# A selective scan on one NeuronCore: every fourth B product of two channel tiles moved from VectorE to ScalarE by way of a transpose, even products kept in SBUF, a third PSUM bank for the side work

## The chip, the cores and the metric

The kernel runs on one core of a Trainium2 chip. The metric is the device time of one execution in microseconds. TensorE is called PE here, VectorE DVE, ScalarE ACT, GpSimd POOL, and SyncE SP; all DMAs of the kernel are issued from SP's queue.

## The reference

The input is x, 8 images of 96 channels, 64 x 64. A vision state-space block comes first, then a small attention and a quantised feed-forward layer. What matters here is the selective scan inside the block. There are 192 inner channels (d), 16 states (n), four directions (k) over the 4,096 pixels (l), and for each of them

```python
delta = softplus(dts + dt_bias)
def step(h, inp):
    u_t, d_t, b_t, c_t = inp
    dA = exp(d_t[..., None] * A)
    h = dA * h + (d_t * u_t)[..., None] * b_t[:, :, None, :]
    y = einsum('bkdn,bkn->bkd', h, c_t)
    return h, y
```

Around the scan stand a layer norm, an input projection with a depthwise 3x3 convolution and SiLU, projections that give dts, B and C, then a norm, a gate, an output projection, two 3x3 convolutions with a channel attention, a linear attention over channels and the feed-forward layer.

## The kernel before

**The scan loop.** Images are taken in pairs (p, four of them). A pair's 2 x 192 channels are three tiles of 128 rows: T = 0 and T = 1 hold the first 128 channels of the one and of the other image, T = 2 the last 64 of both. Time runs in chunks of CH = 1,024 pixels. A *job* is one (p, direction k, chunk ci, tile T); the tiles come in the order 0, 2, 1, and there are 192 jobs. A job has four *groups* (j) of 32 channels, 768 groups in all. A group has four *units* (q = 0 to 3), and a unit is one instruction wide: its 128 partitions are 32 channels times 4 states, so that the four units hold the 16 states. Two units (q = 0, 1 or q = 2, 3) are a *pair*.

For each group PE spreads delta x (tile du, 128 channels) over channel and state: `spread` (L1299) multiplies with a 0/1 matrix into `pu`, two banks of PSUM. For each unit ACT makes da = exp(A delta) (`decay`, L1304); DVE makes the B product pb = pu x bm (L1317), where bm holds four rows of B repeated over the 32 channels; DVE scans, hc = da x h + pb (L1321); POOL copies the last column as the carry for the next chunk and multiplies hc by the C rows, cm (L1331 and the line before). `total` (L1349) adds the four states and four units on PE into `yp`; ACT copies the sum out and SP stores it, or the next direction adds to it.

`pbs` (L437) are two PSUM tiles of two banks each, pu has two, and the banks `pg` and `yp` are the two that all other work shares: eight banks. hc has eight buffers of one unit, bm four and cm five.

**The order.** Each engine's instructions are kept in the order in which the program names them (class `InOrder`; every instruction of the loop therefore has the helper's line, L266, in the profile). The loop (from L1400) goes by pairs: it runs a slot of side work, names `scan(u)`, asks for the next bm (four units ahead) and cm (two ahead), names the next pair's two `decay`, in a group's second pair also the next group's `spread` and the last group's `total`, and runs another slot. So a group has four slots and a job sixteen.

**The side work.** Everything else is written as generators, *lanes*: the projections of the next image pair, the gate, the convolutions, attention and feed-forward of the last one. `Slots` (L283) steps them once a slot. A lane takes one of the two banks with `take` (L301), which asks that a budget of PE and ACT time is positive; RATE (L291) is what each slot adds, CAP the most that is kept. `steps` (L467) prepares the next job: it loads dt rows (`st`) and du, and in slots 6 and 7 makes delta (`dls`, softplus on ACT), multiplies du by it on POOL, and stores delta.

Of the kernel before, what the change touches and what calls it, by code (L numbers as in the profile page):

```python
# [9 lines left out]
F32 = mybir.dt.float32  # L10
# [271 lines left out]

class Slots:  # L283
# [7 lines left out]
    RATE, CAP = (2.0, 1.8), (3.0, 2.4)  # L291

    def __init__(self, *banks):
        self.lanes, self.later, self.first, self.at, self.due = [], [], None, 0, {}
        self.banks, self.held, self.big = banks, set(), set()
        self.left, self.behind = [0.0, 0.0], lambda: False
# [3 lines left out]

    def take(self, pe, act, long=0):  # L301
        while True:
            i = 1 if self.at % 2 and not long else 0


            due = long and (
                self.at % 4 > (long == 2) or self.at % 16 <= 6 < self.at % 16 + long
            )
            if i not in self.held and not due and min(self.left) > (-2 if long else 0):
                self.held.add(i)  # L310
                self.pay(pe, act)
                return self.banks[i]
            yield
# [7 lines left out]
    def give(self, bank):  # L321
        i = self.banks.index(bank)
        self.after(1, lambda: self.held.remove(i))
# [4 lines left out]
    def run(self):  # L328
        self.at += 1
        self.left = [min(v + r, c) for v, r, c in zip(self.left, self.RATE, self.CAP)]  # L330
        for f in self.due.pop(self.at, ()):
            f()
        if self.first is not None and next(self.first, self) is self:
            self.first = None
        order = [self.lanes, self.later]
        for lanes in order[::-1] if self.behind() else order:
            turn = self.at % len(lanes) if lanes else 0
            for lane in lanes[turn:] + lanes[:turn]:
                if next(lane, self) is self:
                    lanes.remove(lane)  # L340

    def idle(self):
        return not (self.lanes or self.later or self.first or self.due)
# [7 lines left out]
def phase_b(  # L351
# [8 lines left out]
    with ExitStack() as ctx:  # L360
# [28 lines left out]
        gmean = cp.tile([C, C], F32, name="gmean")  # L389
        nc.vector.memset(gmean, 1.0 / (C * 128))  # L390
# [35 lines left out]
        hp = inner.enter_context(tc.tile_pool(name="b_h", bufs=8))  # L426
# [10 lines left out]
        pbs = [psc.tile([128, CH], F32, name=f"pb{i}") for i in range(2)]  # L437
# [5 lines left out]
        slots = Slots(bank0, yps)  # L443
# [6 lines left out]
        carries, bcs, dus, dls, sts, das, hcs, prevs, yet = ({} for _ in range(9))  # L450
# [11 lines left out]

        def exps():

            se.preload_act_table_set("natural_log_exp_and_others")

        def steps(job):  # L467

            p, k, ci, c, T, at = where(job)
            if T == 0:  # L470

                sts[job // 3] = gp.tile([32 + 2 * R, 512], F32, name="st")
                r0 = 64 + R * (k // 2)
                for i, hs in enumerate(halves):
                    for b in range(2):
                        nc.sync.dma_start(
                            sts[job // 3][32 * i + R * b : 32 * i + R * b + R, :],
                            xd_d[k % 2][2 * p + b][r0 : r0 + R, at][:, hs],
                        )
            dtw = gp.tile([32 + 2 * R, 128], F32, name="dtw")  # L480
            for i in range(2):
                nc.sync.dma_start(dtw[32 * i : 32 * i + 2 * R, :], a["dtw"][:, k, T, :])
            dus[job] = gp.tile([128, CH], F32, name="du", bufs=2)
            nc.sync.dma_start(dus[job], xi_d[k % 2][p][T][:, at])
            yield

            while slots.at % 16 != 6:
                yield
            dl = gp.tile([128, CH], F32, name="dls")
            for i, hs in enumerate(halves):  # L490
                bank = slots.banks[i]
                assert i not in slots.held
                slots.held.add(i)
                slots.pay(0.9, 2.5)
                rows = slice(32 * i, 32 * i + 2 * R)
                pe.matmul(bank, dtw[rows, :], sts[job // 3][rows, :], start=True, stop=True)
                se.activation(dl[:, hs], bank, AF.Softplus, bias=dtb[:, k, T : T + 1])
                slots.give(bank)
                if i:
                    exps()  # L500
                else:
                    yield
            ge.tensor_mul(dus[job], dus[job], dl)
            yield from wait(2)
            nc.sync.dma_start(dl_d[k][p][T][:, at], dl)
            yield

# [242 lines left out]
        def rest(b, s):  # L750
# [139 lines left out]
            for j in range(8):  # L890
# [17 lines left out]
                h8 = gp.tile([128, 3, 512], F8, name=f"h8{s}")  # L908
# [4 lines left out]
                for i in range(3):  # L913
                    bank = yield from slots.take(0.3, 1.3)
                    pe.matmul(bank, w1q[:, i * 128 : i * 128 + 128], x8, start=True, stop=True)
                    h16 = gp.tile([128, 512], F16, name=f"h16{s}")
# [11 lines left out]
                o16 = gp.tile([128, 512], F16, name=f"h16{s}")[0:C, :]  # L928
# [88 lines left out]
        def before_scans(p):  # L1017
# [26 lines left out]
            def norms(b):  # L1044
# [16 lines left out]
                for j in js:  # L1061
# [16 lines left out]
                    pe.matmul(bank[0:C, 0:4], gmean, cs, start=True, stop=True)  # L1078
                    se.mul(ngm, bank[0:C, 0:4], -1.0)
# [9 lines left out]
                    pe.matmul(bank[0:C, 0:4], gmean, gs, start=True, stop=True)  # L1089
                    se.activation(r, bank[0:C, 0:4], AF.Ln, bias=eps[0:C])  # L1090
# [177 lines left out]
        def weights(u, i):  # L1268
# [6 lines left out]
            if (job // 3, b, q, i) in bcs:  # L1275
                return
            t = bcp.tile([128, CH], F32, name=("bm", "cm")[i], bufs=(4, 5)[i])
            r0 = 32 * (k // 2) + 16 * i + 4 * q
            nc.sync.dma_start(
                t, xd_d[k % 2][2 * p + b][r0 : r0 + 4, at].unsqueeze(0).to_broadcast([32, 4, CH])  # L1280
# [30 lines left out]
        def scan(u):  # L1311
# [3 lines left out]
            step, last = (-1, 0) if k >= 2 else (1, CH - 1)  # L1315
            for i in range(2):
                ve.tensor_mul(pbs[i], pu, bcs[job // 3, batch(u), q + i, 0])  # L1317
            for i in range(2):
                t = hp.tile([128, CH], F32, name="hc")
                carry = carries[p, k][:, T, 4 * j + q + i : 4 * j + q + i + 1]  # L1320
                ve.tensor_tensor_scan(  # L1321
                    t[:, ::step], das.pop(u + i)[:, ::step], (pbs[i])[:, ::step],
                    0.0 if ci == 0 else carry, ALU.mult, ALU.add,
                )
                hcs[u + i] = t
            for i in range(2):
                v = u + i
                carry = carries[p, k][:, T, 4 * j + q + i : 4 * j + q + i + 1]
                if ci < NCH - 1:
                    ge.tensor_copy(carry, hcs[v][:, last : last + 1])  # L1330
                ge.tensor_mul(hcs[v], hcs[v], bcs[job // 3, batch(u), q + i, 1])  # L1331
# [17 lines left out]
        def total(g):  # L1349
# [9 lines left out]
            for n in range(4):  # L1359
                for i in range(4):  # L1360
                    pe.matmul(
                        yp[32 * i : 32 * i + 32, :], add,
                        hcs[4 * g + n][:, 256 * i : 256 * i + 256],
                        start=(n == 0 and k < 2), stop=(n == 3),
                    )
            for n in range(4):
# [33 lines left out]
        for u in range(0, n, 2):  # L1400
# [37 lines left out]
            if q == 2:  # L1438
                if g + 1 < n // 4:
                    spread(g + 1)  # L1440
                if g > 0:
                    total(g - 1)
# [504 lines left out]
```

## Time and profile before

Three runs: 11065.08, 11066.59 and 11072.03 us, median 11066.59. The profiled execution has a span of 11058.4 us from its first to its last instruction; the median is 8.2 us longer.

| engine | busy us | share of the span | instructions |
|---|---|---|---|
| PE | 7887.2 | 71% | 39468 |
| DVE | 10525.7 | 95% | 6651 |
| ACT | 6596.3 | 60% | 9175 |
| POOL | 9028.7 | 82% | 6649 |

| stretch | us | what |
|---|---|---|
| 0 to 214.6 | 214.6 | first images' norms and projections |
| 214.6 to 10724 | 10509 | scan loop |
| 10724 to 11058.4 | 334 | what is left of the last pair |

How to read it: busy is the time in which an engine had at least one instruction under way. A group's row gives the line, the engine, the operation, the tile written and those read, the shape of output and first input, the count, then the busy time, the mean ns of one instruction, and the idle time before them with what ended most of it. The mean granted clock of TensorE is 0.815 of full speed. In a timeline row come the start, the duration in us, the engine, the line, the operation and, behind x, how many instructions in a row it merges.

### The profile page before, as it was taken

To read this page: it belongs to the slowest core of one execution; us is meant where nothing else is said; L and a number is where in the kernel's file an instruction comes from. 1 tells how busy PE (TensorE), PEld (TensorE's weight loads), DVE (VectorE), ACT (ScalarE), POOL (GpSimd) and SP (SyncE) were. 2 spreads that over 40 slices of the span, in tenths; PEclk is the share of its full clock that TensorE was granted. 3 is DMA by queue.
4 is the path that set the end of the run, shared out by engine and by line. 5 is a ranking of instruction groups with operands and counts; after the bars stand their busy time and mean duration, and the time that the engine had idled before them with its cause. 6 is when DMAs were issued, how large, how long until landed. Compare 5 with 4: busy or idle time off the path is not lost.

```text
span 11058.4 us, 128094 instructions
## 1 busy us (share of the span) xinstructions
PE 7887.2 (71%) x39468; PEld 3111.6 (28%) x39468; DVE 10525.7 (95%) x6651; ACT 6596.3 (60%) x9175; POOL 9028.7 (82%) x6649
## 2 busy tenths in 40 slices
PE   7755778655568887767777787776767776665778
PEld 3322333222223332223222332223322222222223
DVE  4999999999999999999999999999999999999974
ACT  2544765544567666556776656565776656665554
POOL 2788877787898888998888887899889888988860
PEclk8877888877788888878878888887878877777889
DMA  3445554454555555666545555566544555644551
GB/s 117 151 165 180 160 156 157 141 188 156 163 185 172 171 172 157 211 214 195 158 152 160 157 178 159 177 220 209 172 157 159 160 164 179 197 157 140 173 157 37
DMA packets 900188, 1834.20 MB, mean 166 GB/s; under 512 B 247965, under 2 KB 421214, under 8 KB 892462
## 3 DMA queue, kind: packets, MB, share of 16 engines
q1 hardware_dynamic: 899502, 1826.01, 52.8%
q8 instruction: 314, 5.14, 0.2%
q14 instruction: 372, 3.05, 0.1%
HBM read 1405.13 MB, written 420.42 MB: 165 GB/s over the span
## 4 chain that ended last, share of the span: by engine, by line
PE 32%; issue 29%; DVE 17%; POOL 11%; ACT 6%; DMA 4%; SPq 0%; DVEq 0%; POOLq 0%; ACTq 0%
PE pu L266 12%; PE yp L266 11%; DVE hc L266 11%; POOL hc L266 7%; PE pg L266 6%; DVE pb L266 5%; ACT u L266 2%; ACT da L266 2%; POOL u L266 2%; PE t L266 2%; PE ps L197 1%; DMA bm<-xd 1%; POOL turn L266 1%; POOL carry L266 1%; ACT L266 1%
## 5 line engine op out<-in xcount | busy, mean ns | idle before, releaser
L266 POOL TENSOR_TENSOR hc<-hc,cm 128x1024 f32<-128x1024 f32 x3072 | 7230.0, 2359 | 591.0 <-DVE hc L266 382.6
L266 DVE TENSOR_TENSOR_SCAN hc<-da,carry,pb 128x1024 f32<-128x1024 f32 x2304 | 5276.8, 2334 | 38.1 <-ACT da L266 31.5
L266 PE MATMUL pu<-du,c_sel 128*128 128x512 f32 x3072 | 2452.5, 944 | 2244.1 <-DVE pb L266 2239.6
L266 DVE TENSOR_TENSOR pb<-pu,bm 128x1024 f32<-128x1024 f32 x3072 | 3601.6, 1220 | 133.9 <-PE pu L266 105.9
L266 ACT ACTIVATE da<-dl,c_alog 128x1024 f32<-128x1024 f32 x3072 | 3352.8, 1140 | 91.4 <-DVE hc L266 73.8
L266 PEld LDWEIGHTS pu<-du,c_sel 128*128 128x128 f32 x3072 | 790.0, 281 | 3521.1 <-DVE pb L266 2784.8
L266 DVE TENSOR_TENSOR_SCAN hc<-da,pb 128x1024 f32<-128x1024 f32 x768 | 1713.1, 2275 | 38.9 <-ACT da L266 22.8
L266 ACT COPY y<-yp 128x256 f32<-128x256 f32 x768 | 284.4, 370 | 2348.9 <-PE yp L266 2198.4
L266 PE MATMUL yp<-hc,c_add 128*32 128x256 f32 x24576 | 1660.8, 416 | 22.6 <-ACT s L266 6.6
L266 PEld LDWEIGHTS yp<-hc,c_add 128*32 128x32 f32 x24576 | 768.6, 120 | 1200.1 <-issue 628.4
L266 POOL COPY carry<-hc 128x1 f32<-128x1 f32 x2304 | 422.5, 183 | 766.1 <-DVE hc L266 744.9
L266 ACT ACT_TABLE_LOAD x566 | 726.2, 1283 | 38.2 <-DMA cb<-zs 16.9
L266 ACT COPY u<-pg 128x512 f32<-128x512 f32 (+6 forms) x397 | 218.3, 550 | 712.3 <-PE pg L266 641.2
L266 POOL TENSOR_TENSOR u<-u,u 96x512 f32<-96x512 f32 (+1 forms) x426 | 537.5, 1269 | 105.9 <-ACT u L266 101.8
L266 POOL TENSOR_TENSOR du<-du,dls 128x1024 f32<-128x1024 f32 x192 | 452.7, 2358 | 91.5 <-ACT dls L266 91.1
L266 ACT COPY u<-yp 96x512 f32<-96x512 f32 (+6 forms) x347 | 188.0, 542 | 465.5 <-PE yp L266 404.5
L266 PE MATMUL pg<-ain,wmain 96*128 96x512 f32 x792 | 354.1, 599 | 0.0
L266 PE MATMUL pg<-ain,wmix 96*128 96x512 f32 x792 | 353.0, 598 | 0.0
L266 PE MATMUL yp<-prev,ident 128*128 128x256 f32 x768 | 321.9, 512 | 39.0 <-ACT u L266 27.4
L266 PEld LDWEIGHTS yp<-prev,ident 128*128 128x128 f32 x768 | 214.5, 283 | 381.8 <-issue 264.3
L266 PE MATMUL pg<-st,dtw 12*128 12x512 f32 x384 | 218.5, 649 | 49.4 <-ACT u L266 28.8
L266 PE MATMUL yp<-st,dtw 12*128 12x512 f32 x384 | 227.9, 674 | 18.3 <-ACT u L266 10.9
(340 smaller groups left out, 7030.2 us busy)
## 6 DMA issues: line engine op xcount, KB each, us to landing
dl<-dl SPq DMA_DIRECT2D x768, 512.0 KB
bm<-xd SPq DMA_DIRECT2D x512, 512.0 KB
cm<-xd SPq DMA_DIRECT2D x512, 512.0 KB
du<-xi SPq DMA_DIRECT2D x192, 512.0 KB
dl<-dls SPq DMA_DIRECT2D x192, 512.0 KB
ya<-y SPq DMA_DIRECT2D x384, 128.0 KB
prev<-ya SPq DMA_DIRECT2D x384, 128.0 KB
xi<-u SPq DMA_DIRECT2D x152, 256.0 KB
```

What stands on the lines that cost most here:

```text
L197: nc.tensor.matmul(bank[r, :].rearrange("p (h w) -> p h w", w=W), w[:, t if len(which) > 1 or w is wmix else 0, columns], pads[b][:, 8 * j ...
L266: op(*args, **kw)
```

## The change

Tiles T = 0 and T = 1 are *woven*; T = 2 is not. In a woven group the product of the last unit (q = 3) is no longer made by DVE. B of that unit is made to be a per-partition scalar instead: `steps` loads four more rows of B for each image (`st` grows to 104 rows), and PE transposes them (into `pt`, a new bank) to `bt`, time on the partitions. Once du is there, `spin` transposes it too, 128 columns at a time, and ACT multiplies each transposed block by four columns of bt, with the four states side by side (tile `turned`, a ring of six, shared with delta). `weave` then has PE turn the part of the group back, eight transposes of 128 x 128, into the odd product's PSUM tile; it is named in a woven group's first pair, behind the next group's spread. The scan of q = 3 reads it there.

The even products' tile pb0 moves from PSUM to SBUF; pb1 stays in PSUM. That and pt leave a bank for a third lane bank, `ph`. In a woven group the third product (q = 2) is made between the first two scans, and the spread of the next group moves to the first pair. hc and cm become tiles of a pair: hc four of them (as many units as before), cm two (four units where there were five), and POOL's two products and two carry copies of a pair become one of each. Budgets rise from (2.0, 1.8) to (2.2, 2.0) a slot, and `take` picks the bank that has rested longest. The tiles h8 and h16 of the feed-forward share the buffers of others, gmean goes (its factor moves into two ACT instructions), and the program is built with dynamic_dma_scratch_size=1024.

The core of the diff:

```diff
-    RATE, CAP = (2.0, 1.8), (3.0, 2.4)
+    RATE, CAP = (2.2, 2.0), (4.0, 4.0)
...
-        hp = inner.enter_context(tc.tile_pool(name="b_h", bufs=8))
+        hp = inner.enter_context(tc.tile_pool(name="b_h", bufs=4))
...
-        pbs = [psc.tile([128, CH], F32, name=f"pb{i}") for i in range(2)]
+        bank2 = psc.tile([128, 512], F32, name="ph")
+        turning = psc.tile([128, 512], F32, name="pt")
+        pbs = [wp.tile([128, CH], F32, name="pb0", bufs=1), psc.tile([128, CH], F32, name="pb1")]
...
+        def woven(job):
+            return jobs[job][3] < 2
...
+            if T == 0:
+                bts[job // 3] = gp.tile([128, 8, 8], F32, name="bt", bufs=2)
+                yield
+                for i in range(2):
+                    r, at8 = slice(64 + 32 * i, 72 + 32 * i), 256 * i
+                    for x in range(4):
+                        pe.transpose(
+                            turning[:, at8 + 8 * x : at8 + 8 * x + 8],
+                            sts[job // 3][r, 128 * x : 128 * x + 128],
+                            ident[r, r],
+                        )
+                    se.copy(bts[job // 3][:, 4 * i : 4 * i + 4, :], turning[:, at8 : at8 + 32])
...
+        def spin(job):
+            turns[job], b = [], jobs[job][3]
+            bt, nxt = bts[job // 3], slots.at + 1
+            while len(turns[job]) < 4:
+                n, at = len(turns[job]), slots.at % 16
+                if slots.at < nxt or (job and woven(job - 1) and n >= EXTRA and 3 < at < 14):
+                    yield
+                    continue
+                nxt = slots.at + 2 - (at >= 14 or at < 3)
+                slots.pay(0.4, 2.9)
+                bank = turning[:, 256 * (n % 2) : 256 * (n % 2) + 256]
+                for i in range(2):
+                    x = 128 * (2 * n + i)
+                    pe.transpose(bank[:, 128 * i : 128 * i + 128], dus[job][:, x : x + 128], ident)
+                t = gp.tile([128, 2, 128, 4], F32, name="turned", bufs=RING)
+                for i in range(2):
+                    for m in range(4):
+                        c = 4 * b + m
+                        se.mul(
+                            t[:, i, :, m], bank[:, 128 * i : 128 * i + 128],
+                            bt[:, 2 * n + i, c : c + 1],
+                        )
+                turns[job].append(t)
+                yield
+
+        def weave(g):
+            job, j, _ = units[4 * g]
+            for x in range(8):
+                t = turns[job][x // 2][:, x % 2].rearrange("p c n -> p (c n)")
+                pe.transpose(
+                    pbs[1][:, 128 * x : 128 * x + 128], t[:, 128 * j : 128 * j + 128], ident
+                )
...
-            for i in range(2):
-                ve.tensor_mul(pbs[i], pu, bcs[job // 3, batch(u), q + i, 0])
...
+            def product(i, to):
+                ve.tensor_mul(pbs[to], pu, bcs[job // 3, batch(u), q + i, 0])
+
+            if not (woven(job) and q):
+                product(0, 0)
+                product(1, 1)
             for i in range(2):
                 ve.tensor_tensor_scan(
-                    t[:, ::step], das.pop(u + i)[:, ::step], (pbs[i])[:, ::step],
-                    0.0 if ci == 0 else carry, ALU.mult, ALU.add,
+                    t[:, i, ::step], das.pop(u + i)[:, ::step], pbs[i][:, ::step],
+                    0.0 if ci == 0 else carry[:, i : i + 1], ALU.mult, ALU.add,
                 )
...
+                if woven(job) and q == 0 and i == 0:
+                    product(2, 0)
+            if ci < NCH - 1:
+                ge.tensor_copy(carry, t[:, :, last])
+            ge.tensor_mul(t, t, bcs[job // 3, batch(u), q, 1])
...
-            if q == 2:
-                if g + 1 < n // 4:
-                    spread(g + 1)
-                if g > 0:
-                    total(g - 1)
+            if (q == 0) == woven(units[u][0]) and g + 1 < n // 4:
+                spread(g + 1)
+            if q == 0 and woven(units[u][0]):
+                assert len(turns[units[u][0]]) == 4
+                weave(g)
+            if q == 2 and g > 0:
+                total(g - 1)
```

## The prediction

> **What bounds the kernel now.** I read the page's busy times first, then the costliest groups, then the busy times of the scan loop alone (its first product starts at 214.57, its last POOL product ends near 10724), then the timeline of one stretch. From the page:
>
> ```profile
> PE 7887.2 (71%) x39468; PEld 3111.6 (28%) x39468; DVE 10525.7 (95%) x6651; ACT 6596.3 (60%) x9175; POOL 9028.7 (82%) x6649
> ...
> L266 POOL TENSOR_TENSOR hc<-hc,cm 128x1024 f32<-128x1024 f32 x3072 | 7230.0, 2359 | 591.0 <-DVE hc L266 382.6
> L266 DVE TENSOR_TENSOR_SCAN hc<-da,carry,pb 128x1024 f32<-128x1024 f32 x2304 | 5276.8, 2334 | 38.1 <-ACT da L266 31.5
> ...
> L266 DVE TENSOR_TENSOR pb<-pu,bm 128x1024 f32<-128x1024 f32 x3072 | 3601.6, 1220 | 133.9 <-PE pu L266 105.9
> ```
>
> DVE is the bound: scans and B products fill it, with little idle time before them. Busy times in the loop (columns PE, PEld, DVE, ACT, POOL, clock, DMA):
>
> ```profile
> 214.50:10724.00 10509.50, 7459.90 (x37794) 2932.34 (x37798) 10318.60 (x6150) 6404.01 (x8841) 8960.88 (x6598) 0.81 0.54 170
> ```
>
> The loop takes 10,509 us, 768 groups of four units, 13.68 us each; head and tail are the other 549. DVE's own cadence, in its timeline:
>
> ```profile
> 5003.50 4.57 DVE L266 TENSOR_TENSOR_SCAN hc<-da,carry,pb 128x1024 f32<-128x1024 f32 x2
> 5007.99 2.34 DVE L266 TENSOR_TENSOR pb<-pu,bm 128x1024 f32<-128x1024 f32 x2
> 5010.24 4.58 DVE L266 TENSOR_TENSOR_SCAN hc<-da,carry,pb 128x1024 f32<-128x1024 f32 x2
> ```
>
> Start to start, two products take 2.25 and two scans 4.49: 1.12 a product, 2.245 a scan. Scans without a carry start 2.19 apart (4.38 for two).
>
> **What decides: where the scan's inputs lie.** Today pb is in PSUM, so a scan and a product each read one tensor from SBUF, and POOL does not disturb them, though it is busy 85% of the loop: the scan with a carry has 2310/2335/2366 as its shortest, median and longest ns. The change puts the even products into SBUF; an even scan then reads two tensors there, da and pb0. The loop has no such DVE instruction, but the start of the program has. DVE's timeline, then POOL's:
>
> ```profile
> 13.56 1.47 DVE L135 TENSOR_TENSOR s<-s,tmv 128x9 f32<-128x9 f32 x1
> ...
> 15.20 1.43 DVE L128 TENSOR_TENSOR q<-q 128x9 f32<-128x9 f32 x1
> ...
> 16.83 0.10 DVE L129 TENSOR_TENSOR q<-q,tmv 128x9 f32<-128x9 f32 x1
> ```
> ```profile
> 13.38 1.63 POOL L146 TENSOR_TENSOR xt<-xt,m 128x864 f32<-128x864 f32 x1 [3.17 <-DVE m L126]
> 14.96 1.64 POOL L147 TENSOR_TENSOR xt<-xt,r 128x864 f32<-128x864 f32 x1
> ```
>
> Nine elements from two SBUF tensors take 0.10 us alone and 1.4 beside POOL, and end at 15.03 and 16.63: 0.02 and 0.03 after POOL's instructions (15.01, 16.60). A large one is put off as well: xn<-xt,tmv 128x768 takes 0.94 alone and 1.73 when it starts inside a POOL instruction, ending 0.81 after it. So such an instruction waits until the running POOL instruction is through. That DVE's turn also keeps POOL out, and that a scan behaves like a plain product, no row shows.
>
> The Trainium skill, "SBUF — State Buffer", section "Who interferes with whom", speaks against this change: any DVE instruction with two SBUF inputs and a POOL instruction that reads SBUF exclude each other for a whole instruction. By it the turns below add up; by the rows' narrower reading only plain products wait, and rival 2 holds.
>
> **The change, part by part.**
>
> *DVE's products.* Two thirds of the groups (512) lose one product: 512 x 1.12 = 575 us saved on the path as it is now. An even product written to SBUF I leave at 1.12 (the 128x768 products SBUF to SBUF run at 0.94/768 = 1.22 ns an element, the present ones at 1.19: within 0.03 either way, 0.03 x 1,024 ns = 30 ns). The scan runs at 2.2 ns an element whatever feeds it: no change of its own rate.
>
> *POOL.* A product of 512 elements takes 1.27 and one of 1,024 2.36, so 1.09 per 512 and 0.18 fixed; a pair is 0.18 + 4 x 1.09 = 4.54. 1,536 pairs = 6,973 against 7,230; carry copies halve from 2,304 to 1,152 of 0.183, saving 211. POOL in the loop: 8,961 - 257 - 211 = 8,493.
>
> *Turns.* 1,536 even scans, three quarters of 2.245 and a quarter of 2.19, are 3,427 us in which POOL may not read. If the two take turns all the time, the loop lasts 8,493 + 3,427 = 11,920 instead of 10,509. Do they? In a pair with a carry POOL holds 0.27 (carry copy, start to start) + 4.54 = 4.8; after its even scan DVE needs an odd scan and two products, 2.245 + 2.25 = 4.5, or 3.4 in the middle of a woven group. So DVE asks 0.3 to 1.4 us before POOL is done and the next pair's product lies ready behind: no time is free. Small terms: a restart of POOL after each even scan, valued at 0.1 (its gap between copy and product is 0.27 - 0.18 = 0.09; ends 0 and 0.2): 154; the gap itself, 1,152 x 0.08: 92. Turns lost to a late DVE (rival 1) in one pair of twenty: 77 x (9.3 - 7.05) = 173. Loop: 11,920 + 154 + 92 + 173 = 12,339.
>
> The low end: POOL seems to claim its turn a little after its recorded start (s<-s,tmv at 27.59 takes 0.13, although a POOL product is recorded from 27.57). With 0.1 us free in each of 1,152 + 1,536 + 1,222 = 3,910 instructions the sum falls by 391, to 11,529.
>
> *ScalarE.* 128 woven jobs x 32 = 4,096 products of 128x128 from PSUM. Rows: u<-yp 96x128 268 ns, starting 0.255 apart; u<-u,small 96x128, with a pointer operand, 0.39 apart. I take 0.36 (a pointer operand costs 0.09: turn<-turn,dsum 128x512 takes 718 ns, u<-u 96x512 without one 630), 1,475 us, between 1,044 and 1,600. ACT rises from 6,404 to 7,900 in the loop, off the path. The three products that follow one another before T = 0 stand ahead of the next da; 8.7 us of them delay a da by about 1 us, 64 times: covered by the turns, 64 us if that cover is gone.
>
> *PE.* 4,096 + 1,024 transposes; the nearest rows, four transposes of 128x96 in 0.60 or one each 0.11 us, give 0.15 each, 770 us in all, twice that at the low clock. PE rises from 7,460 to 8,230 to 9,000 of 12,339: off the path on average. The wait it adds: the last scan of a woven group waits for eight transposes (0.27 + 7 x 0.11 = 1.0, up to 2), which wait behind the spread of the next group. That one takes 1.96 at the high clock and 3.78 after a pause (the median pu matmul, 1061 ns against 590 at best, says mostly 3.78). DVE's scan before it, 2.245 plus its wait for POOL, covers this; uncovered it costs about 1 us x 512.
> The Trainium skill, "TensorE: Matmul & The Clock Gate", Part 4, says that transposes do not lift the clock and take about 275 ns each in a kernel; by that eight are 2.2 us in a row, by the rows 1.0. Neither changes the sum while POOL sets it.
>
> *Queues.* 256 more small loads of st rows, 0.32 to 0.5 us each on SP, about 100 us beside a queue that waits. cm has four buffers for five, so the first C rows of a new batch wait for POOL's last use, and later issues queue behind; 128 times between 0 and the longest such wait of now, 2.9 us (371 in all); I take 0, since POOL is one pair late anyway. Third bank, larger budgets, reused u tiles, scales moved into operands: they move lane work, which has more time per slot than before; 0, up to the 106 us that DVE waits for pu now.
>
> **Sum.** 549 + 12,339 = 12,888 of span, against 11,058; the median of the runs is 8 us above the span. Forecast 12,900.
>
> **Rivals.**
> 1. *DVE misses its turn.* When a transpose, da or spread makes DVE more than 0.3 us late, POOL starts the next pair first. Then a pair is 4.8 + 2.245 + 2.245 = 9.3 in T = 2 groups (18.6 a group); a woven group is one missed turn, 17.4 (scan, POOL's 4.8 twice, scan, product and scan: 2.25 + 9.6 + 2.25 + 1.12 + 2.25). In every group: 512 x 17.4 + 256 x 18.6 = 13,670, + 557 = 14,230; in half of them about 13,550. For: the 0.3. Against: POOL's lane work (1,222 instructions) makes POOL later, and the scan after the odd one in a woven group needs no product, so DVE is first there.
> 2. *A scan takes no turn* (faster). Place: DVE's second input; decides at all 1,536 even scans. Loop 10,509 - 575 = 9,934, + 549 + 8 = 10,490; if the cold spread delays each woven group by 1 us, 11,000. Value 10,700. For: no scan with two SBUF inputs is in the trace. Against: the rows above.
> 3. *No turns, but PE late*: the same with weave and lanes over 1.12 us a group: 11,070 to 11,400.
>
> **Chances.** Forecast 0.55, rival 1 0.26, rival 2 0.16, rival 3 0.03. The range takes in the forecast's low end (11,529 + 557 = 12,086) and rival 1 in nearly all groups: 12,050 to 14,100. Faster by over 0.2% 0.16, within 0.2% (all that a measurement here can tell from no change) 0.01, slower 0.83.
>
> **What would show it.** Right: even scans with recorded times spread from 2.3 to 7 us, odd ones constant; POOL products of 4.5 to 7; POOL plus even scans near the loop's length; ACT and PE below 75%. Wrong: even scans at 2.3 throughout. Rival 1: POOL idle for 2 us or more after most pairs.

## The result, and the profile after

The changed kernel takes 13,779.01 us (median of four runs, 13,753.90 to 13,791.22) against 11,066.63: the ratio is 1.2449, 95% interval 1.2431 to 1.2466. The profiled execution took 13,777.25 us and has a span of 13,775.5. The forecast was 12,900; the result lies 879 above it and 451 below rival 1 in every group (14,230), so nearer to the rival.

First the page of the changed kernel: the busy times, then the groups that answer to those shown of before.

```profile
PE 8978.3 (65%) x45100; PEld 3964.6 (29%) x45100; DVE 12350.5 (90%) x6138; ACT 7766.6 (56%) x13451; POOL 10863.7 (79%) x3961
...
L266 POOL TENSOR_TENSOR hc<-hc,cm 128x2048 f32<-128x2048 f32 x1536 | 7301.5, 4755 | 957.9 <-DVE hc L266 710.6
L266 DVE TENSOR_TENSOR_SCAN hc<-da,carry,pb 128x1024 f32<-128x1024 f32 x2304 | 7085.3, 3105 | 722.3 <-ACT da L266 427.5
...
L266 DVE TENSOR_TENSOR pb<-pu,bm 128x1024 f32<-128x1024 f32 x2560 | 3017.2, 1210 | 132.0 <-PE pu L266 85.6
L266 DVE TENSOR_TENSOR_SCAN hc<-da,pb 128x1024 f32<-128x1024 f32 x768 | 2223.3, 2926 | 238.2 <-ACT da L266 141.6
...
L266 POOL COPY carry<-hc 128x2 f32<-128x2 f32 x1152 | 1208.9, 1049 | 1348.1 <-DVE hc L266 1255.2
```

DVE makes 512 products fewer and is busy 1,825 us longer. The products fell by 584; the scans rose by 2,319 (a scan with a carry from 2,334 to 3,105 ns at the mean), the rest by 90. DVE's idle time, span less busy, rose from 533 to 1,425. 1,825 and 892 are the 2,717 us between the spans. A carry copy on POOL takes 1,049 ns where it took 183, for two columns.

The busy times of the scan loop (PE, PEld, DVE, ACT, POOL, clock, DMA):

```profile
226.00:13440.00 13214.00, 8546.11 (x43404) 3781.45 (x43405) 12142.44 (x5637) 7562.69 (x13083) 10797.23 (x3910) 0.78 0.44 136
```

The loop has grown by 2,705, head and tail hardly. The prediction's 8,493 us of work on POOL are recorded as 10,797: waits for a turn are recorded inside the instruction.

A stretch of T = 2, DVE's timeline and then POOL's:

```profile
5004.54 2.33 DVE L266 TENSOR_TENSOR pb<-pu,bm 128x1024 f32<-128x1024 f32 x2
5006.78 6.89 DVE L266 TENSOR_TENSOR_SCAN hc<-da,carry,pb 128x1024 f32<-128x1024 f32 x2
5013.59 2.33 DVE L266 TENSOR_TENSOR pb<-pu,bm 128x1024 f32<-128x1024 f32 x2
5015.84 6.88 DVE L266 TENSOR_TENSOR_SCAN hc<-da,carry,pb 128x1024 f32<-128x1024 f32 x2
```
```profile
5004.76 4.53 POOL L266 TENSOR_TENSOR hc<-hc,cm 128x2048 f32<-128x2048 f32 x1 [1.32 <-DVE hc L266]
5009.23 2.19 POOL L266 TENSOR_TENSOR small<-small 96x4 f32<-96x4 f32 x1
5011.38 2.36 POOL L266 TENSOR_TENSOR du<-du,turned 128x1024 f32<-128x1024 f32 x1
5013.81 4.52 POOL L266 TENSOR_TENSOR hc<-hc,cm 128x2048 f32<-128x2048 f32 x1
5022.94 4.52 POOL L266 TENSOR_TENSOR hc<-hc,cm 128x2048 f32<-128x2048 f32 x1 [4.61 <-DVE hc L266]
```

A pair lasts 9.05 us, not 6.74 as before and not 7.05 as forecast. POOL starts a pair's product as soon as the odd scan is through (5004.76). DVE's two products are done 2.25 later, and the even scan, asked for at 5006.78, stands until POOL's product ends at 5009.29. While that scan runs, four columns of 96 rows keep POOL 2.19 us: the scan shuts POOL out as well. After the odd scan it is POOL's turn again. The forecast had POOL's product run beside the odd scan and the next two products; here it runs beside the two products alone, and the even scan waits for the rest of it.

Over the whole trace the even scans are recorded at 2.26 to 12.02 us (mean 3,809 ns) and the odd ones at 2.25 to 2.35 (mean 2,313).

### The profile page after: what moved, and what is told of

It reads as the page before. It is cut to its first block, busy times and chain, and to the rows that moved or that the text cites. A ratio compares the mean times of both kernels' runs of the same rounds, so it can differ in the third digit from the quotient of the medians.

```text
span 13775.5 us, 137230 instructions
## 1 busy us (share of the span) xinstructions
PE 8978.3 (65%) x45100; PEld 3964.6 (29%) x45100; DVE 12350.5 (90%) x6138; ACT 7766.6 (56%) x13451; POOL 10863.7 (79%) x3961
## 3 DMA queue, kind: packets, MB, share of 16 engines
q8 instruction: 356, 5.83, 0.2%
## 4 chain that ended last, share of the span: by engine, by line
issue 26%; POOL 25%; PE 20%; DVE 17%; ACT 9%; DMA 3%; SPq 0%; POOLq 0%; DVEq 0%; ACTq 0%
DVE hc L266 14%; POOL hc L266 14%; PE pu L266 7%; PE yp L266 4%; POOL carry L266 4%; POOL u L266 3%; DVE pb L266 3%; PE ph L266 2%; ACT u L266 2%; ACT turned L266 2%; ACT da L266 2%; PE pb L266 2%; PE pg L266 2%; POOL du L266 2%; POOL turn L266 2%
## 5 line engine op out<-in xcount | busy, mean ns | idle before, releaser
L266 POOL TENSOR_TENSOR hc<-hc,cm 128x2048 f32<-128x2048 f32 x1536 | 7301.5, 4755 | 957.9 <-DVE hc L266 710.6
L266 DVE TENSOR_TENSOR_SCAN hc<-da,carry,pb 128x1024 f32<-128x1024 f32 x2304 | 7085.3, 3105 | 722.3 <-ACT da L266 427.5
L266 DVE TENSOR_TENSOR pb<-pu,bm 128x1024 f32<-128x1024 f32 x2560 | 3017.2, 1210 | 132.0 <-PE pu L266 85.6
L266 DVE TENSOR_TENSOR_SCAN hc<-da,pb 128x1024 f32<-128x1024 f32 x768 | 2223.3, 2926 | 238.2 <-ACT da L266 141.6
L266 POOL COPY carry<-hc 128x2 f32<-128x2 f32 x1152 | 1208.9, 1049 | 1348.1 <-DVE hc L266 1255.2
L266 ACT ACTIVATE turned<-pt,bt 128x128 f32<-128x128 f32 x4096 | 1177.7, 502 | 690.9 <-PE pt L266 336.8
L266 POOL TENSOR_TENSOR u<-u,u 96x512 f32<-96x512 f32 (+1 forms) x474 | 1009.9, 2137 | 28.2 <-ACT u L266 24.4
L266 PEld LDWEIGHTS pb<-ident,turned 128*128 128x128 f32 x4096 | 661.2, 182 | 540.3 <-DVE hc L266 296.8
L266 PE MATMUL pb<-ident,turned 128*128 128x128 f32 x4096 | 715.0, 333 | 32.7 <-DVE hc L266 32.3
L266 POOL TENSOR_TENSOR du<-du,turned 128x1024 f32<-128x1024 f32 x192 | 553.0, 2880 | 107.7 <-ACT turned L266 83.3
```

Of the source, the lines that this page charges most:

```text
L266: op(*args, **kw)
```

## The experiments

Theory T: from the even products' place in SBUF on, even scans and POOL's instructions take turns, and turns missed by DVE make the rest. Rivals are told with each run. "Busy" and "idle" are DVE's, in the profiled execution (idle is span less busy):

| kernel | us | ratio, 95% interval | busy | idle |
|---|---|---|---|---|
| before (as predicted from) | 11,067 | | 10,526 | 533 |
| after | 13,779 | 1.2449 (1.2431 to 1.2466) | 12,351 | 1,425 |
| 1 place alone | 12,795 | 1.1561 (1.1527 to 1.1594) | 11,743 | 1,049 |
| 2 no C product | 11,716 | 1.0586 (1.0555 to 1.0617) | 10,163 | 1,548 |
| 3 C product by unit | 12,899 | 1.1655 (1.1621 to 1.1689) | 11,252 | 1,647 |
| 4 scan after scan | 13,841 | 1.2505 (1.2456 to 1.2554) | 12,144 | 1,716 |
| 5 place in PSUM | 11,875 | 1.0725 (1.0707 to 1.0743) | 10,089 | 1,792 |
| 6 one woven tile | 11,432 | 1.0325 (1.0310 to 1.0340) | 10,313 | 1,122 |
| 7 no ACT products | 11,534 | 1.0420 (1.0405 to 1.0436) | 10,162 | 1,364 |
| 8 no weave | 11,454 | 1.0346 (1.0331 to 1.0362) | 10,132 | 1,333 |
| 9 decays ahead | 11,743 | 1.0607 (1.0591 to 1.0623) | 10,206 | 1,536 |
| 10 budgets alone | 11,094 | 1.0022 (1.0012 to 1.0032) | 10,527 | 561 |
| 11 one tile, decays ahead | 11,553 | 1.0436 (1.0421 to 1.0452) | 10,315 | 1,247 |
| 12 lanes before spread | 11,386 | 1.0286 (1.0269 to 1.0303) | 10,135 | 1,248 |

**1. The place alone.** The kernel before with one line of the change (and its smaller scratch for DMAs):

```diff
-pbs = [psc.tile([128, CH], F32, name=f"pb{i}") for i in range(2)]
+pbs = [wp.tile([128, CH], F32, name="pb0", bufs=1), psc.tile([128, CH], F32, name="pb1")]
```

> The kernel before with one thing changed: the even products' tile pb0 lies in SBUF instead of PSUM (and dynamic_dma_scratch_size=1024). Theory T (turns: a scan with two SBUF inputs and a POOL instruction that reads SBUF exclude each other): POOL's 8,961 us in the loop and 3,427 us of even scans add up to 12,388; with the 557 outside, 12,950 to 13,400. Rival S (the place of pb0 costs nothing; the new chains of the change, da behind the turned products and the last scan behind the transposes, make DVE late): no change, 11,030 to 11,110.

12,795 us, 155 under T's range and far from the rival: the line costs 1,727. (The smaller scratch was not run by itself, but 5 has it too, without long scans.) The busy times of its page, then a stretch of POOL's timeline:

```profile
PE 8232.4 (64%) x39468; PEld 3175.6 (25%) x39468; DVE 11743.3 (92%) x6651; ACT 6613.3 (52%) x9175; POOL 11652.5 (91%) x6649
```
```profile
5000.34 0.18 POOL L266 COPY carry<-hc 128x1 f32<-128x1 f32 x1
5000.60 2.34 POOL L266 TENSOR_TENSOR hc<-hc,cm 128x1024 f32<-128x1024 f32 x1
5002.90 2.18 POOL L266 COPY carry<-hc 128x1 f32<-128x1 f32 x1
```

One carry copy takes 0.18, the next 2.18: an even scan runs in it. POOL goes from 9,029 to 11,652 busy with the same instructions. Here the turns are used well: the median pair of T = 2 takes 7.14 us from odd scan to odd scan. The span, 12,792, is 145 below the sum of POOL's work, the even scans and the rest (8,961 + 3,427 + 549 = 12,937), 0.09 for each of the 1,536 even scans. The trace has it too: the even scans that waited (1,177 recorded above 2.6 us) end 2.15 us after the end of POOL's instruction, where two scans in a row with a carry start 2.245 apart. The prediction's low end had such an overlap.

**2. No C product.** The changed kernel without POOL's product with C.

```diff
-            ge.tensor_mul(t, t, bcs[job // 3, batch(u), q, 1])
```

> The changed kernel without POOL's product with C (hc goes to the sums unmultiplied; the carry copies, and POOL's other work stay). Theory T: POOL has some 1,500 us left in the loop, even scans fall back to a median and mean near 2.3, and the time is DVE's own sum and some waits for da and transposes: 10,500 to 11,000. Rival S: POOL is not in DVE's chain, DVE stays late: 13,200 to 13,780.

11,716: 2,063 go with the product, but 649 more than before stay, against both expectations. Against before, the products fell by 579, the scans rose by 123, the rest by 93, and the idle time by 1,015. The even products still lie in SBUF here, and the median even scan takes 2,340 ns as before: two inputs from SBUF alone do not make a scan longer. DVE's waits in this kernel (in all, times, longest; before had 54.3 for da):

```profile
DVE hc L266 <- ACT da L266: 621.9, 342, 7.1
DVE hc L266 <- PE pb L266: 197.3, 266, 2.9
DVE hc L266 <- PE yp L266: 162.8, 79, 6.6
DVE pb L266 <- PE pu L266: 157.6, 74, 31.0
```

So a second loss lies beneath the turns, in what ACT and PE bring late. Experiments 5 to 12 are after that.

**3. C product by unit.** The changed kernel, with POOL's paired product as two.

```diff
-            ge.tensor_mul(t, t, bcs[job // 3, batch(u), q, 1])
+            for i in range(2):
+                ge.tensor_mul(t[:, i, :], t[:, i, :], bcs[job // 3, batch(u), q, 1][:, i, :])
```

> The changed kernel with POOL's product with C made for each unit (two of 1,024 elements) instead of once for a pair. Theory T: a turn that DVE misses costs 2.3 us instead of 4.5, so although POOL has 1,536 x 0.18 = 276 us more to do, the time falls towards the sum of turns, 8,769 + 3,427 + 557 = 12,750: 12,750 to 13,300. Rival S: no gain, 13,700 to 13,850.

12,899, as T expected: splitting POOL's instruction brings 880 us. From the ends of DVE's scans in the trace I worked out how long each of the 512 pairs of T = 2 lasted, and called it missed above 8.5 us. In the changed kernel 72% are missed, here 23%, in experiment 1 21%. In the changed kernel a miss is followed by a miss in 92% of 321 cases and a pair in time by a miss in 28% of 127; here it is 18% and 21%, in experiment 1 21% and 21%. (Pairs above 8.5 us have other causes too: they are 2% in before and 9% in 2, where no C product is there to wait for.) With the paired product, missing a turn lasts.

**4. Scan after scan.** The changed kernel, with the even product of the next pair named between the scans of the pair before, so that DVE asks for its turn straight after an odd scan, while POOL has not begun.

```diff
-            if not (woven(job) and q):
+            if q == 0 and u not in early:
                 product(0, 0)
+            if q == 0:
                 product(1, 1)
...
-                if woven(job) and q == 0 and i == 0:
+                if q == 0 and i == 0:
                     product(2, 0)
+                if q and i == 0 and not woven(job):
+                    product(1, 1)
+                if q and i == 0 and woven(job) and u + 2 < len(units):
+                    v = u + 2
+                    ve.tensor_mul(pbs[0], pu, bcs[units[v][0] // 3, batch(v), 0, 0])
+                    early.add(v)
```
(The third product is then made in every group's first pair.)

> The changed kernel with DVE's order altered and nothing else: each even scan follows the odd scan before it directly (in T = 2 groups the third product is made between the first two scans and the fourth between the last two; behind a woven group the next group's first product is made before the last scan), so that DVE asks for its turn before POOL gets the pair. Theory T with missed turns as the cause of the forecast's shortfall: most of the 880 us between forecast and result go, 12,600 to 13,200. If missed turns are not it, or rival S: 13,600 to 13,900.

13,841, a miss. DVE's timeline, then POOL's, over one group of T = 2:

```profile
5015.00 2.36 DVE L266 TENSOR_TENSOR pb<-pu,bm 128x1024 f32<-128x1024 f32 x2 [1.42 <-PE pu L266]
5017.73 4.48 DVE L266 TENSOR_TENSOR_SCAN hc<-da,carry,pb 128x1024 f32<-128x1024 f32 x1 [0.37 <-PE yp L266]
5022.24 1.22 DVE L266 TENSOR_TENSOR pb<-pu,bm 128x1024 f32<-128x1024 f32 x1
5023.39 4.58 DVE L266 TENSOR_TENSOR_SCAN hc<-da,carry,pb 128x1024 f32<-128x1024 f32 x2
5027.88 1.21 DVE L266 TENSOR_TENSOR pb<-pu,bm 128x1024 f32<-128x1024 f32 x1
5029.19 2.35 DVE L266 TENSOR_TENSOR_SCAN hc<-da,carry,pb 128x1024 f32<-128x1024 f32 x1
5032.96 2.36 DVE L266 TENSOR_TENSOR pb<-pu,bm 128x1024 f32<-128x1024 f32 x2 [1.42 <-PE pu L266]
```
```profile
5015.51 4.55 POOL L266 TENSOR_TENSOR hc<-hc,cm 128x2048 f32<-128x2048 f32 x1
5025.89 10.91 POOL L266 TENSOR_TENSOR hc<-hc,cm 128x2048 f32<-128x2048 f32 x2 [5.83 <-DVE hc L266]
```

DVE now goes straight through the middle of the group (the even scan there takes no longer than the odd ones), but POOL stands 5.83 us idle meanwhile and does both products at its end; the next group's first scan meets the second of them and takes 4.48, and the spread comes 1.42 late. The group still lasts 17.96. The turn missed in the middle moved to the boundary: of the pairs of T = 2 a pair in time is now followed by a miss in 86% of 202 cases, a miss by a miss in 18% of 246.

**5. The place in PSUM.** The changed kernel with both pb in PSUM. The two banks for it are those of ph and pt, so spins and the transposes of bt go through a lane bank, with larger budgets, and the lanes have two banks, with the old rule of choosing between them.

```diff
-        bank2 = psc.tile([128, 512], F32, name="ph")
-        turning = psc.tile([128, 512], F32, name="pt")
-        pbs = [wp.tile([128, CH], F32, name="pb0", bufs=1), psc.tile([128, CH], F32, name="pb1")]
+        pbs = [psc.tile([128, CH], F32, name=f"pb{i}") for i in range(2)]
...
-    RATE, CAP = (2.2, 2.0), (4.0, 4.0)
+    RATE, CAP = (3.2, 3), (5, 5)
```

> The whole idea of the change with the even products left in PSUM: the woven tiles keep their transposes and ScalarE products, the paired POOL product stays, but there is no bank for lanes and none for turning, so that the spins go through a lane bank (larger budgets of 3.2 and 3.0 us a slot). Theory T (the turns between scan and POOL cost most, and waits for ScalarE and PE cost DVE another microsecond or so in every woven group): no turns here, so scans at 2.31 to 2.37 throughout; 11,067 - 584 for the products + about 1,000 of waits, as without POOL's product = 11,300 to 11,700. Rival S (with the turns gone nothing else is lost, and the 1,015 us of DVE waiting seen without POOL's product came from the SBUF place too): 10,500 to 10,700.

11,875, 175 above T's range. From its page:

```profile
L266 DVE TENSOR_TENSOR_SCAN hc<-da,carry,pb 128x1024 f32<-128x1024 f32 x2304 | 5309.7, 2334 | 945.3 <-ACT da L266 473.4
```

Scans with a carry are back at 2,334 ns, with POOL's paired product in place. With 1 and 2, the place and POOL's work together are the cause of the long scans; and the change doesn't pay without them either. DVE is busy 437 less than before and idle 1,259 more. Its longest waits, in all: 586 us for da (54 before), 437 for hc buffers (yp), 199 for pu (106 before), 147 for the weave.

**6. One woven tile.** As 5, with T = 1 alone woven (budgets 2.6 and 2.4, at most 4).

```diff
-            return jobs[job][3] < 2
+            return jobs[job][3] == 1
```

> As the run before it in this call, with even products in PSUM, but only tile T = 1 woven, so that a woven job never follows a woven one and ScalarE makes 2,048 products, not 4,096 (budgets 2.6 and 2.4). 256 products are saved, 287 us. Theory T with waits in proportion to woven groups: 11,067 - 287 + 500 = 11,200 to 11,350. Theory T with the waits only where two woven jobs follow each other and ScalarE's products crowd: 10,800 to 10,950, faster than the kernel before. Rival S: 10,750 to 10,800.

11,432, above all three ranges: half of the woven groups bring a little under half of 5's loss (361 of 804 us), so it isn't only where woven jobs follow each other (the two runs' budgets differ as well). DVE is busy 212 less, and idle 589 more.

**7. No ACT products.** As 2; ACT's 4,096 products are left out too, and PE weaves from one constant tile. (The ring of `turned` tiles, then delta's alone, has three places, not six.)

```diff
-                t = gp.tile([128, 2, 128, 4], F32, name="turned", bufs=RING)
-                for i in range(2):
-                    for m in range(4):
...
-                turns[job].append(t)
+                turns[job].append(still)
```

> The changed kernel without POOL's product with C, and without ScalarE's products for the woven tiles: PE transposes into the lane of turning as before and weaves from one constant tile (both kinds of product are left out of the computation). Beside 11,716 us with ScalarE's products. If ScalarE's batches of products are what makes da late (DVE waits 622 us for da there, 54 in the kernel before): 11,000 to 11,200. If PE's transposes and the weave are the cause: 11,500 to 11,720.

11,534: 182 less than 2, just inside what was expected if PE is the cause. ACT does some 1,065 us less and da is still waited for 466 us, against 54 before. ACT's own products are the smaller part of the 649.

**8. No weave.** As 2, without the eight transposes back.

```diff
-                weave(g)
+                pass
```

> The changed kernel without POOL's product with C, and without the weave: ScalarE makes its products, PE transposes delta x, but the eight transposes back per woven group are left out and the last scan of the group reads what lies in the bank (both are left out of the computation). Beside 11,716 us with the weave. If ScalarE's products delay da by themselves, only the waits for the weave and for the spread behind it go (197 + 158 - 106 us): 11,350 to 11,550. If the weave is what holds PE, DVE and so ScalarE: 10,700 to 11,100.

11,454: 262 less than 2, the size of DVE's waits for the weave and a little; 586 us of waits for da stay. The time is in the first alternative's range, but the reason given there, ACT's products, accounts for only 182 us by 7.

The trace of 2 then showed where. I took the time of each group from the ends of its scans: in woven jobs the third group takes 15.9 and 15.8 us at the mean (T = 0, T = 1), in T = 2 14.7; in before all third groups take 13.5 to 13.6. Slots 6 and 7, in which delta is made, lie in the second group. The first softplus on ACT, in before and then in 2 (its tile is called turned there); the last columns are ACT's idle time ahead of it:

```profile
L266 ACT ACTIVATE dls<-pg,c_dtb 128x512 f32<-128x512 f32 x192 | 131.9, 687 | 6.9 <-PE pg L266 4.6
```
```profile
L266 ACT ACTIVATE turned<-pg,c_dtb 128x512 f32<-128x512 f32 x192 | 132.0, 687 | 487.8 <-PE yp L266 315.3 <-PE pg L266 171.4
```

Nearly all of it is in woven jobs: of 521 us ahead of both softplus instructions 279 lie in T = 0, 216 in T = 1 and 26 in T = 2. One such place, on PE and then on ACT:

```profile
2631.06 3.78 PE L266 MATMUL pu<-du,c_sel 128*128 128x512 f32 x4 [5.97 <-DVE pb L266]
2634.64 1.36 PE L266 MATMUL pb<-ident,turned 128*128 128x128 f32 x8
2635.93 0.69 PE L266 MATMUL pg<-st,dtw 12*128 12x512 f32 x1
...
2638.41 0.96 PE L266 MATMUL yp<-prev,ident 128*128 128x256 f32 x2 [1.35 <-ACT turned L266]
```
```profile
2637.09 0.69 ACT L266 ACTIVATE turned<-pg,c_dtb 128x512 f32<-128x512 f32 x1 [8.18 <-PE yp L266]
...
2639.67 2.19 ACT L266 ACTIVATE da<-dl,c_alog 128x1024 f32<-128x1024 f32 x2
```

In a woven group's first pair the next group's spread now waits on PE for DVE's third product (5.97), runs for 3.78 after that pause, and the weave follows. Delta's matmuls stand behind both; ACT stands 8.18 for them, with da and the y copies queued behind. The weave is the smaller part of this: with it left out (8), ACT still stands idle 340 us ahead of the first softplus, and the third group of woven jobs still takes 15.6 and 16.0. With ACT's products left out (7) it takes 16.3 and 16.2. What both keep is the early spread, which waits for DVE. `total` needs the bank that softplus reads (1.35), and so the hc buffers come free late. No lane had work in this place; where one has, it stands in the same queues.

**9. Decays ahead.** As 2, with the da of the next group's first pair named one pair earlier in woven groups, ahead of the lanes.

```diff
-            for v in range(u + 2, min(u + 4, n)):
-                decay(v)
+            for v in range(u + 2, min(u + (6 if q == 0 and woven(units[u][0]) else 4), n)):
+                if v not in das:
+                    decay(v)
```

> The changed kernel without POOL's product with C (left out of the computation), and with the two exponentials for the next group's first pair issued at the first step of a woven group, ahead of the lanes' ScalarE work of the next two slots, not behind it. Beside 11,716 us without that. Theory Q (da is late because those lanes stand on PE behind the spread of the next group and the eight transposes, and da stands on ScalarE behind the lanes): the 622 us in which DVE waits for da fall to 150 or less, the time to 11,150 to 11,300. Rival: lanes with larger budgets or ScalarE's products hold da up wherever it stands: 11,550 to 11,720.

11,743, no gain, against theory Q. The waits for da fell from 622 to 365 and those for hc buffers (yp) rose from 163 to 420; ACT now waits 569 us in da for DVE to free a buffer (139 in 2). I read it so: whatever stands behind the wait is late, and moving one thing ahead of it moves the loss to the next.

**10. Budgets alone.** The kernel before with the new RATE and CAP.

```diff
-    RATE, CAP = (2.0, 1.8), (3.0, 2.4)
+    RATE, CAP = (2.2, 2.0), (4.0, 4.0)
```

> The kernel before with the changed kernel's budgets for the lanes alone (2.2 and 2.0 us a slot, at most 4.0 saved up, in place of 2.0, 1.8, 3.0 and 2.4). Theory Q (the order on PE makes da late, not the budgets): within 40 us of the kernel before. Rival (larger lots of lane work delay da and the spread): 11,200 or more.

11,094, 26 us more, an interval of 0.12 to 0.32%. By themselves the budgets are not the cause.

**11. One woven tile, decays ahead.** 6 with the edit of 9.

> Even products in PSUM, only T = 1 woven, two lane banks (11,432 us), with the same earlier place for the two exponentials in woven groups. Theory Q: of 285 us in which DVE waits for da some 230 go: 11,150 to 11,250, still above the kernel before, since the waits for pu and yp (235 and 147 us) stay. Rival: 11,400 to 11,450.

11,553, 121 slower than 6. The waits for da fell from 285 to 248 only, those for yp rose from 147 to 282. A second miss for Q.

**12. Lanes before the spread.** As 2, but in a woven group's first pair the slot of side work goes ahead of spread and weave on PE, and delta is begun one slot earlier, so that both its matmuls stand ahead of a spread (the rule that keeps bank pg free for delta moves by a slot with it).

```diff
-            while slots.at % 16 != 6:
+            while slots.at % 16 != 5:
...
+            if q == 0 and woven(units[u][0]):
+                slots.run()
             if (q == 0) == woven(units[u][0]) and g + 1 < n // 4:
                 spread(g + 1)
...
-            slots.run()
+            if q or not woven(units[u][0]):
+                slots.run()
```

> The changed kernel without POOL's product with C (left out of the computation), and with the lanes' slot of a woven group's first step issued on PE ahead of the early spread and the weave, not behind them, and the two delta matmuls one slot earlier, so that both stand ahead of a spread (slots 5 and 6, not 6 and 7). Beside 11,716 us. In that kernel the third group of a woven job takes 15.9 us at the mean, the other woven groups 13.7 to 15.4, and ScalarE stands idle 488 us ahead of its softplus instructions, 7 in the kernel before. Theory P (PE's order: delta matmuls and lanes stand behind the spread, which waits for DVE, and behind the eight transposes; ScalarE stands idle for them with da and the y copies queued behind): ScalarE's idle time ahead of the softplus falls under 150 us, the third group to 13.7 or less, the time to 11,250 to 11,450. Rival (ScalarE and PE have no time left in a woven group, wherever their work stands): 11,600 to 11,750.

11,386, 330 less than 2, as theory P expected. ACT's rows:

```profile
L266 ACT ACT_TABLE_LOAD x962 | 1234.2, 1283 | 38.0 <-DMA cb<-y 17.2 <-PE pg L266 3.4 <-PE yp L266 0.6
...
L266 ACT ACTIVATE turned<-pg,c_dtb 128x512 f32<-128x512 f32 x192 | 132.0, 687 | 46.1 <-PE pg L266 44.0
```

The idle time ahead of softplus falls from 488 to 46, the third group of woven jobs to 13.8 and 13.7 (13.7 or less was expected), and the waits for yp from 163 to 38. That holds although ACT has more to do: with da's exponentials between the two softplus instructions it loads a function table 962 times (618 in 2), 441 us more. The first groups gain too (15.4 and 14.2 to 13.8 and 13.4), the second lose (13.9 and 14.1 to 14.3 and 15.2), and the waits for the weave rise from 197 to 335. The lanes' move and delta's were not run apart.

## Why the prediction was right, and where it was wrong

**Right: the bound, the place, the turns.** DVE sets the pace, and its even scans wait for POOL once their second input lies in SBUF: 1,727 us for that line (1), scans at 2,334 ns again without it (5), and even scans at a median of 2,340 ns without POOL's product (2). Both open points of that step are settled: the scan behaves like a product, and it keeps POOL out in turn. The section "Who interferes with whom" of the Trainium skill's page "SBUF — State Buffer", by which a DVE instruction with two SBUF inputs and a POOL instruction that reads SBUF exclude each other for their whole length, agrees with (1): a one-column copy takes 0.18 us alone and 2.18 beside an even scan. Rivals 2 and 3 fall with (1). Of the signs named ahead, the spread of the even scans beside constant odd ones came; POOL's work and the even scans together, 11,920 by the sum, are 1,294 short of the loop.

**Right in size:** the products saved are 584 us, worked out as 575. The paired product at 4.54 stands in the timeline at 4.52 and 4.53. The restart of 0.1 at each even scan has the wrong sign, 0.09 of overlap by (1), some 290 us less in all.

**Mis-sized: "Turns lost to a late DVE (rival 1) in one pair of twenty", 173.** The loop is 13,214 against the 12,339 of the sum, 875 more. By groups: the sum gave 16.07 a group; T = 2 groups take 17.89 (256 x 1.82 = 466) and woven ones 16.86 (512 x 0.79 = 404), together 870. 72% of the pairs of T = 2 miss their turn, not 5%: what was priced as rival 1, at a chance of 0.26, is what most of these pairs do, and the range held only because it was drawn to take rival 1 in. The margin of 0.3 us was seen; what I missed is that a missed turn isn't an event that passes. Once POOL is level with DVE, its product starts when the odd scan ends, the next even scan asks 2.25 us later and waits out the 4.5, and POOL is level again. By these times only lane work that keeps POOL some 2.25 us beyond the odd scan's end brings the good order back (an argument from the timeline, not a run). The persistence is in the trace (92% after 28%), and (3) shows that it hangs on the size of POOL's instruction: with two products of 2.3 for one of 4.5, the even scan gets in between them, and the median pair of T = 2 takes 7.03. That costs 880 us, the size of the error. In part the match is chance: the sum's 290 too much for the restart and DVE's waits for da (569 us, 54 before), which it took as covered, stand in the same difference. The reason "for" in rival 1 was right; its "against", that POOL's lane work keeps POOL behind, holds only until DVE is late once. (4) shows that asking earlier does not mend it as long as POOL's two products of a group come in one lot.
What I had put down as a sign for rival 1, POOL idle after most pairs, shows in only 492 of 1,536 (1,255.2 + 710.6 us in 321 and 171 waits): in 486 of the others POOL goes from one pair's product to the next with no lane work and no wait, and in 490 lane work stands in that place, which an even scan can lengthen (the 96 x 4 elements above).

**Wrong, and hidden by the turns: ACT and PE "off the path", the delay of da "covered".** Without the C product the kernel loses 649 us (2), where rival 2 has it win 575. The prediction's own prices without that cover, 64 us for da and 512 for the weave, would make it 11,066, not 11,716. The 0.36 for an ACT product was too much (eight take 2.30 in the timeline, 0.29 each), and a weave takes 1.40 us on PE (715.0 us for 512), between the 1.0 from the rows and 2.2, the estimate from the 275 ns of the Trainium skill's "TensorE: Matmul & The Clock Gate", Part 4. One transpose is recorded at 273 ns at the median, but eight in a row overlap. The durations were not the fault. The step that failed is the wait: I named what waits for the weave (the last scan) and not what is queued behind spread and weave on PE, the lanes' matmuls and delta's, and behind those on ACT, da and the y copies. Another order brings 330 us (12), though 12 pays for more table loads. Beside it, each taken out of 2 by itself, the weave costs 262 (8) and ACT's products 182 (7). How the three add up wasn't tried, and 12 still has 335 us of waits for the weave and 415 for da, whose cause stays open. So does how much of the 649 the changed kernel pays on top of its turns: its waits for da are 569, but a late DVE and a late POOL cost the same microsecond only once. The changed kernel with the order of 12 wasn't tried either.

**The expected gain.** No version beat the kernel before. Of those that save products and leave nothing out of the computation, 6 is the nearest, at 1.0325.

## What to carry to other kernels

Before a tensor moves from PSUM to SBUF, list which instructions then read two SBUF tensors, and what POOL does in that time: one such line cost 16% here. Where two engines take turns, ask not only who comes first but what state a missed turn leaves behind; a longer instruction on one side can make one miss last. And when a waiting instruction moves to an earlier place in an engine's order, follow everything named behind it, through the next engine's queue too.

## What the runs showed of the hardware that was not expected

- An instruction of POOL on 96 x 4 elements took 2.19 us beside an even scan, and 1,152 carry copies of two columns 1,049 ns at the mean: the length of the other side's instruction counts, not one's own.
- An even scan starts about 0.09 us before POOL's recorded end (1).
- ACT loads a function table in 1.283 us. The third lane bank lets lane work with another function in between the two softplus instructions: 618 loads in the changed kernel, 566 before and again in 5 with two lane banks, 67 us in all. ACT's timeline in 2, where it happens:

```profile
3858.78 1.28 ACT L266 ACT_TABLE_LOAD   x1
3860.07 0.69 ACT L266 ACTIVATE u<-ph,eps 128x512 f32<-128x512 f32 x1
3860.78 1.28 ACT L266 ACT_TABLE_LOAD   x1
```

- The mean granted clock of TensorE was 0.785 in the changed kernel (0.815 before), with PE busy 65%, and 0.831 in 2 with 73%.
